# Attention kernel: sums of exponentials by a DMA transpose and VectorE sums instead of matmuls with ones

## The chip, the core and the metric

The kernel runs on one core of a Trainium2 chip. The metric is device time in microseconds (us) for one launch. TensorE (PE in the profile) does the matmuls, ScalarE (ACT) the exponentials, VectorE (DVE) elementwise work, sums and evacuations, GpSimd (POOL) some elementwise work, and SyncE (SP) issues most of the DMA transfers.

## The reference

The layer is group norm, one linear map to queries, keys and values, attention with 8 heads of 64 channels over 2304 positions, an output projection and a residual, for 4 images.

```python
b, c, h, w = 4, 512, 48, 48          # t = 2304 positions, d = 64
hn  = group_norm(x, 32 groups) * gn_scale + gn_bias
qkv = einsum('oc,bchw->bohw', qkv_w, hn) + qkv_b        # then float16
w   = softmax(einsum('bhct,bhcs->bhts', q * scale, k * scale), axis=-1)
a   = einsum('bhts,bhcs->bhct', w, v)
out = x + einsum('oc,bchw->bohw', proj_w, a) + proj_b
```

The softmax needs, for every head and query t, the sum over all 2304 keys s of exp(score). This change concerns only how that sum is formed.

## The kernel before

Two heads ("a pair") are worked on together: 4 images x 4 pairs = 16 pairs g. The queries of a pair are cut into 5 blocks j, four of 512 queries and one of 256: 80 blocks. A block's keys are worked through in steps of three score tiles: 6 steps for a block of 512, 3 for one of 256; 432 steps in all ("stream"). Scores are computed as keys x queries: the keys lie on the 128 partitions, the queries along the row. So the sum over keys is a sum over partitions plus a sum over tiles.

```python
P, D, QB, BURST, BEHIND = 128, 64, 512, 3, 2
ppool = tc.tile_pool(name="ppool", bufs=3)
work  = tc.tile_pool(name="work", bufs=2)
small = tc.tile_pool(name="small", bufs=2)
ps_s  = tc.tile_pool(name="ps_s", bufs=3, space=PSUM)
ps_av = tc.tile_pool(name="ps_av", bufs=1, space=PSUM)   # products with v, and the sums
ps_w  = tc.tile_pool(name="ps_w", bufs=1, space=PSUM)    # other work: q, k, v, projection

def scores(u):                       # one step: 6 matmuls and 3 exponentials
    pt = ppool.tile([P, BURST, 2, QB], F16, tag="p")
    for r in range(BURST):
        ps = ps_s.tile([P, 2, QB], F32, tag="ps")
        ...
                    nc.tensor.matmul(ps[:, h, ...], kt[rows, ...], qt[rows, o : o + n], ...)  # L932
        nc.scalar.activation(pt[:, r], ps, AF.Exp)                                            # L939

def values(u):                       # exponentials times v, two steps behind
    ...
                    nc.tensor.matmul(av[0][lo : lo + D, :n], vv[...], pt[:, r, h, ...], ...)  # L957
    if last and u is not stream[-1]:
        avx[g, j] = work.tile([P, QB], F32, tag="avx")
        nc.vector.tensor_copy(avx[g, j][:, :n], av[0][:, :n])                                 # L966

def add(u):                          # exponentials of the steps added up, elementwise
    ...
    t = acc[g, j][0]                 # [P, BURST, 2, QB] float16, one buffer
    nc.vector.tensor_tensor(t, before, pt, ALU.add)                                           # L986
    if last:
        for r in range(1, BURST):
            nc.vector.tensor_tensor(t[:, 0], t[:, 0], t[:, r], ALU.add)                       # L989
        acc[g, j] = [t[:, :1]]

def add_up(g, j, bank=None, more=False):        # sum over partitions by ones on TensorE
    sl = ps_av.tile([P, QB], F32, tag="av")     # (or the bank given)
    ...
            nc.tensor.matmul(sl[lo : lo + D, :n], ones16, t[:, r, h, ...], ...)               # L1009
    return sl

def rows(g, j, sl):                  # out of PSUM, and one row of each head to 128 partitions
    sx = work.tile([P, QB], F32, tag="rows")
    nc.vector.tensor_copy(sx[:, :n], sl[:, :n])                                               # L1025
    sm = small.tile([P, 2, QB // P], F32, tag="sums")
    for h in range(2):
        nc.sync.dma_start(sm[:, h, : n // P], sx[h * D : h * D + 1, :n])                      # L1028
    ...

def invert(g, j):
    nc.vector.reciprocal(inv[:, :, :per], sums[g, j][:, :, :per])                             # L1054
    nc.sync.dma_start(row[:, :n].rearrange("h (p i) -> p h i", i=per), inv[:, :, :per])       # L1056

def spread(g, j):                    # each head's row to its 64 partitions
    nc.sync.dma_start(ib[h * D : (h + 1) * D, :n], row[h : h + 1, :n].to_broadcast((D, n)))   # L1066

def divide(g, j):
    nc.gpsimd.tensor_tensor(atts[g][:, o : o + n], avx..., ibs..., ALU.mult)                  # L1073
```

The linear maps for later pairs and images and the projections of earlier images are cut into pieces, and `fill` puts them between the steps; each piece ends with an evacuation of its PSUM bank by VectorE (L719 for q and k, L768 for v, L864 for the projection). `fill` also gives VectorE statistics and normalization of the next image ("tasks"), with less room at the steps near a block's end. The order of issue, one turn for each step n, `block_at(m)` being the block that ended at step m:

```python
for n in range(end):
    while loads and loads[0][0] <= n:          # x, residuals, outputs, on SP
        loads.popleft()[1]()
    summed = block_at(n - BEHIND - 1)
    if summed:
        rows(*summed, add_up(*summed))
    scores(stream[n])
    if n > 0:
        add(stream[n - 1])
    if summed:
        fill(n)
    if n >= BEHIND:
        values(stream[n - BEHIND])
    if block_at(n - BEHIND - 2):
        check_sums(...); invert(...)           # check_sums: a range check of the sums on GpSimd
    if block_at(n - BEHIND - 3):
        spread(...)
    if block_at(n - BEHIND - 4):
        divide(...)
    if not summed:
        fill(n)
    ...                                        # the last three blocks are summed by add_up here and below
```

Of the kernel before, what the change touches and what calls it, by code (L numbers as in the profile page):

```python
# [12 lines left out]
F32 = mybir.dt.float32  # L13
F32R = mybir.dt.float32r
F16 = mybir.dt.float16
I32 = mybir.dt.int32
AF = mybir.ActivationFunctionType
ALU = mybir.AluOpType
AX = mybir.AxisListType
# [7 lines left out]
P = 128  # L27
# [6 lines left out]
BEHIND = 2  # L34
# [8 lines left out]
QB = 512  # L43
QBLOCKS = [(o, min(QB, T - o)) for o in range(0, T, QB)]
NQ = len(QBLOCKS)
# [422 lines left out]
def fast_path(  # L468
# [12 lines left out]
    nc = tc.nc  # L481
# [3 lines left out]
    xpool = ctx.enter_context(tc.tile_pool(name="xpool", bufs=1))  # L485
# [4 lines left out]
    work = ctx.enter_context(tc.tile_pool(name="work", bufs=2))  # L490
    small = ctx.enter_context(tc.tile_pool(name="small", bufs=2))
# [415 lines left out]


    open_sums = set()
    av, acc, pts, avx, sums, rowd, ibs = {}, {}, {}, {}, {}, {}, {}  # L910

    stream = []
    for g in range(NG):
# [54 lines left out]
    def add(u):  # L968

        g, j, k, last = u  # L970
        pt = pts[u]
        if k == 0:
            acc[g, j] = [pt]
            return
        if j >= NQ - 2 and g == NG - 1 and (last or j == NQ - 1):
            acc[g, j].append(pt)
            return
        before = acc[g, j][0]
        if k == 1:
            acc[g, j] = [  # L980
                work.tile(
                    [P, BURST, 2, QB], F16, tag="acc", bufs=1, name=f"acc_{g}_{j}"
                )
            ]
        t = acc[g, j][0]
        nc.vector.tensor_tensor(t, before, pt, ALU.add)  # L986
        if last:
            for r in range(1, BURST):
                nc.vector.tensor_tensor(t[:, 0], t[:, 0], t[:, r], ALU.add)  # L989
            acc[g, j] = [t[:, :1]]  # L990

    def add_up(g, j, bank=None, more=False):


        o, n = QBLOCKS[j]
        per = QB // n
        sl = bank
        if bank is None:
            sl = ps_av.tile([P, QB], F32, tag="av", name=f"sl_{g}_{j}")
        steps = [  # L1000
            (t, r, a)
            for t in acc.pop((g, j))
            for r in range(t.shape[1])
            for a in range(per)
        ]
        for i, (t, r, a) in enumerate(steps):
            for h in range(2):
                lo = h * D
                nc.tensor.matmul(  # L1009
                    sl[lo : lo + D, :n],  # L1010
                    ones16,
                    t[:, r, h, a * n : (a + 1) * n],
                    start=(i == 0 and (g, j) not in open_sums),
                    stop=(i == len(steps) - 1 and not more),
                )
        if more:
            acc[g, j] = []
            open_sums.add((g, j))
        return sl

    def rows(g, j, sl):

        o, n = QBLOCKS[j]
        sx = work.tile([P, QB], F32, tag="rows", name=f"slx_{g}_{j}")
        nc.vector.tensor_copy(sx[:, :n], sl[:, :n])  # L1025
        sm = small.tile([P, 2, QB // P], F32, tag="sums", name=f"sums_{g}_{j}")
        for h in range(2):
            nc.sync.dma_start(sm[:, h, : n // P], sx[h * D : h * D + 1, :n])  # L1028
        sums[g, j] = sm
        return sx  # L1030

    def divide_here(g, j, source, products, engine):
        o, n = QBLOCKS[j]
        inv = work.tile([P, QB], F32, tag="rows", name=f"inv_{g}_{j}")
        nc.vector.reciprocal(inv[:, :n], source[:, :n])
        engine.tensor_tensor(
            atts[g][:, o : o + n], products[:, :n], inv[:, :n], ALU.mult
        )

    def check_sums(g, j):  # L1040
        n = QBLOCKS[j][1]
        sm = sums[g, j][:, :, : n // P]
        ok = fine.rearrange("p (h i) -> p h i", h=2)[:, :, : n // P]
        for op, limit in ((ALU.is_ge, SUM_MIN), (ALU.is_le, SUM_MAX)):
            t = small.tile([P, 2, QB // P], F32, tag="in", name=f"in_{g}_{j}")
            t = t[:, :, : n // P]
            nc.gpsimd.tensor_scalar(t, sm, limit, None, op)  # L1047
            nc.gpsimd.tensor_tensor(ok, ok, t, ALU.mult)

    def invert(g, j):  # L1050
        n = QBLOCKS[j][1]
        per = n // P
        inv = small.tile([P, 2, QB // P], F32, tag="inv", name=f"inv_{g}_{j}")
        nc.vector.reciprocal(inv[:, :, :per], sums[g, j][:, :, :per])  # L1054
        row = dram.tile([2, QB], F32, tag="row", name=f"row_{g}_{j}")
        nc.sync.dma_start(  # L1056
            row[:, :n].rearrange("h (p i) -> p h i", i=per), inv[:, :, :per]
        )
        rowd[g, j] = row

    def spread(g, j):
        n = QBLOCKS[j][1]
        row = rowd.pop((g, j))
        ib = work.tile([P, QB], F32, tag="rows", name=f"ib_{g}_{j}")
        for h in range(2):
            nc.sync.dma_start(  # L1066
                ib[h * D : (h + 1) * D, :n], row[h : h + 1, :n].to_broadcast((D, n))
            )
        ibs[g, j] = ib

    def divide(g, j):
        o, n = QBLOCKS[j]
        nc.gpsimd.tensor_tensor(  # L1073
            atts[g][:, o : o + n],
            avx.pop((g, j))[:, :n],
            ibs.pop((g, j))[:, :n],
            ALU.mult,
        )
# [37 lines left out]
    def do_tasks(room):  # L1116
        while tasks and tasks[0][0] <= now[0] and room > 0:
            _, us, run = tasks.popleft()
            run()
            room -= us  # L1120
# [18 lines left out]
    def ready(b, j):  # L1139

        if b < B - 1:
            return BEHIND + 6
        return BEHIND + (4 if j == NQ - 3 else 5)

    def put_convert(b, j):
        end = ends[((b + 1) * NPAIR - 1) * NQ + j]
# [16 lines left out]
    for b in range(B):  # L1163
        g = b * NPAIR
# [118 lines left out]
    def fill(n):  # L1283

        idle = beside and beside[0][4] and not beside[0][4]()
        if ended(n - 1):
            room = 1.1 if idle else 0.0  # L1290
        elif ended(n - BEHIND - 1):
            room = 1.1 if idle else 0.5
        else:
            room = 2.4 if idle else 1.1
        do_tasks(room)
        rate, work = 0.0, 0.0
        for us, _, _, _, _, _, need in beside:
            work += us
            left = min(need * per_pair, len(stream) - 4) - n
            rate = max(rate, work / max(left, 1))  # L1300
        credit[0] = min(credit[0] + rate, 4.0)
        closed = False
        while beside:
            us, _, first, last, when, after, _ = beside[0]
            if after > n or (first and closed) or (when and not when()):
                break
            if us > 0.1 and credit[0] < us / 2:
                break
            issue()
            closed = closed or last  # L1310
# [11 lines left out]
    ended = lambda n: 0 <= n < len(stream) and stream[n][3]  # L1322
# [5 lines left out]
    def block_at(n):  # L1328

        return stream[n][:2] if ended(n) and n not in soon else None  # L1330

    for n in range(end):
        now[0] = n
        while loads and loads[0][0] <= n:
            loads.popleft()[1]()
        summed = block_at(n - BEHIND - 1)
        if summed:
            rows(*summed, add_up(*summed))
        wanted(stream[n][0])
        scores(stream[n])  # L1340
        if n > 0:
            add(stream[n - 1])
        if summed:

            fill(n)
        if n >= BEHIND:
            values(stream[n - BEHIND])
        if block_at(n - BEHIND - 2):
            check_sums(*block_at(n - BEHIND - 2))
            invert(*block_at(n - BEHIND - 2))  # L1350
        if block_at(n - BEHIND - 3):
            spread(*block_at(n - BEHIND - 3))
        if block_at(n - BEHIND - 4):

            divide(*block_at(n - BEHIND - 4))
        if not summed:
            fill(n)
        if n - BEHIND in soon:
            g, j = stream[n - BEHIND][:2]
            sx = rows(g, j, add_up(g, j))  # L1360
            if n - BEHIND == soon[1]:
                divide_here(g, j, sx, avx[g, j], nc.gpsimd)
        if n - BEHIND - 1 == soon[0]:
            check_sums(g, j)
            invert(g, j)
        if n - BEHIND - 2 == soon[0]:
            spread(g, j)
            divide(g, j)
    g, b, j = NG - 1, B - 1, NQ - 1
    n = QBLOCKS[j][1]  # L1370
# [9 lines left out]
    add_up(g, j, sl)  # L1380

    every = fine.shape[1] + n
    fines = work.tile([P, QB], F32, tag="rows", name="fines")[:, :every]
    ok = work.tile([P, QB], F32, tag="avx", name="ok")[:, :n]
    nc.scalar.copy(fines[:, :n], sl[:, :n])
    nc.gpsimd.tensor_scalar(ok, fines[:, :n], SUM_MIN, None, ALU.is_ge)
# [83 lines left out]
```

## Time and profile before

| | before |
|---|---|
| time, median of 3 runs | 1618.3 us (1618.05 to 1618.92) |
| span of the profiled run | 1617.1 us, 28315 instructions |
| mean granted TensorE clock | 0.999 |
| DMA | 82.11 MB, mean 51 GB/s |
| exponentials, L939 | 1296 x 1027 ns = 1231.9 us of ScalarE |
| additions of exponentials, L986 | 349, about 1.8 us each, 623.5 us of VectorE |
| matmuls with ones, L1009 | 234, 33.96 us in the records of TensorE |

The busy shares are those of the records: matmuls overlap, so the time that a record of a matmul covers is longer than what the matmul adds to the chain of work that ended last. In the chain, each stretch of time belongs to one instruction only. In a row of the groups, the first numbers are busy time and the mean duration of one, and behind the second bar stands the idle time of the engine just before them and what ended it. In the DMA issues, the last number is the median time from issue to landing.

### The profile page before, as it was taken

The page shows a single profiled execution, that of the slowest core. Times are in us where ns is not written, and L with a number is a line of the kernel's source. Part 1 is how long each engine was busy: PE and PEld are TensorE (multiplying, and loading weights), DVE is VectorE, ACT ScalarE, POOL GpSimd, SP SyncE. Part 2 cuts the span into 40 slices and gives each one's busy share as a digit, 9 for nine tenths or more (in the row PEclk, how much of TensorE's full clock was granted, in tenths as well). Part 3 has the DMA queues.
Part 4 walks back from the last instruction along what each step waited for, and adds up shares of the span by engine and source line. Part 5 has one row for each costly group of instructions (what it writes and reads, how often), then busy time and mean ns, then how long its engine had stood idle before and what let it go on. Part 6 is the DMA issues. An engine that isn't in the chain of part 4 may idle for free.

```text
span 1617.1 us, 28315 instructions
## 1 busy us (share of the span) xinstructions
PE 1583.4 (98%) x11500; PEld 695.5 (43%) x11500; DVE 1136.2 (70%) x1302; ACT 1282.8 (79%) x1398; POOL 298.4 (18%) x419
## 2 busy tenths in 40 slices
PE   6999999999999999999999999999999999999996
PEld 2533434443333534555333353455533334434544
DVE  6267668866666678986666666898666666767775
ACT  3077777888888888888887887887888888888894
POOL 1001102211121222212111121111211131111211
PEclk9999999999999999999999999999999999999999
DMA  7002020000000023511000002352100000016424
GB/s 221 1 14 66 11 64 24 18 14 11 14 18 14 12 65 118 154 54 28 14 11 18 14 12 61 100 158 73 31 14 12 14 18 15 15 24 191 121 62 132
DMA packets 94898, 82.11 MB, mean 51 GB/s; under 512 B 50852, under 2 KB 60964, under 8 KB 94756
## 3 DMA queue, kind: packets, MB, share of 16 engines
q1 hardware_dynamic: 92724, 78.35, 17.3%
q8 instruction: 92, 1.51, 0.4%
q10 hardware_dynamic: 1904, 1.84, 0.4%
q14 instruction: 50, 0.41, 0.1%
q0 software_dynamic: 128, 0.01, 0.0%
HBM read 60.70 MB, written 19.17 MB: 49 GB/s over the span
## 4 chain that ended last, share of the span: by engine, by line
PE 91%; ACT 4%; issue 2%; DVE 1%; DMA 1%; POOL 0%; SPq 0%; ACTq 0%; DVEq 0%; POOLq 0%
PE pqk L709 29%; PE ps L932 19%; PE av L957 19%; PE pv L760 16%; PE pr L837 7%; ACT p L939 3%; PE ps L709 1%; PE sl L1009 1%; ACT a L831 1%; DMA x<-x_dram 1%; DVE acc L986 0%; DMA sums<-slx 0%; DVE r L860 0%; DMA row<-inv 0%; DMA ib<-row 0%
## 5 line engine op out<-in xcount | busy, mean ns | idle before, releaser
L939 ACT ACTIVATE p<-ps 128x1024 f16<-128x1024 f32 x1296 | 1231.9, 1027 | 299.9 <-PE ps L932 299.3
L986 DVE TENSOR_TENSOR acc<-acc,p 128x3072 f16<-128x3072 f16 x270 | 485.3, 1798 | 75.5 <-ACT p L939 74.7
L709 PE MATMUL pqk<-x,wqkv 128*64 128x512 f32 (+1 forms) x2464 | 519.3, 551 | 0.0
L932 PE MATMUL ps<-q,k 64*128 64x512 f16 (+1 forms) x2880 | 359.5, 358 | 6.2 <-ACT p L939 5.3
L957 PE MATMUL av<-p,v 128*64 128x512 f16 (+1 forms) x2880 | 361.0, 364 | 0.4 <-DVE slx L1025 0.3
L760 PE MATMUL pv<-wqkv,x 128*64 128x256 f32 x2304 | 268.6, 380 | 0.0
L709 PEld LDWEIGHTS pqk<-x,wqkv 128*64 128x64 f32 x2464 | 168.9, 137 | 224.2 <-issue 166.8
L1047 POOL TENSOR_SCALAR in<-sums 128x8 f32<-128x8 f32 (+1 forms) x158 | 116.6, 738 | 795.0 <-DMA sums<-slx 788.7
L932 PEld LDWEIGHTS <-k 64*128 64x128 f16 x2880 | 107.3, 94 | 286.1 <-issue 238.1
L957 PEld LDWEIGHTS <-v 128*64 128x64 f16 x2880 | 131.9, 109 | 210.8 <-issue 166.6
L1073 POOL TENSOR_TENSOR att<-avx,ib 128x512 f16<-128x512 f32 (+1 forms) x78 | 120.0, 1539 | 450.4 <-DMA ib<-row 406.3
L760 PEld LDWEIGHTS pv<-wqkv,x 128*64 128x64 f32 x2304 | 160.1, 137 | 92.8 <-issue 4.5
L986 DVE TENSOR_TENSOR acc<-p,p 128x3072 f16<-128x3072 f16 x79 | 138.2, 1749 | 0.0
L837 PE MATMUL pr<-a,whi 128*128 128x512 f32 (+1 forms) x312 | 122.2, 399 | 4.6 <-DVE r L860 3.2
L837 PE MATMUL pr<-a,wlo 128*128 128x512 f32 (+1 forms) x312 | 114.4, 373 | 0.0
L989 DVE TENSOR_TENSOR acc<-acc 128x1024 f16<-128x1024 f16 x156 | 108.4, 695 | 5.4
L719 DVE TENSOR_SCALAR q<-pqk,bqkv 128x512 f16<-128x512 f32 (+1 forms) x79 | 55.0, 696 | 80.4 <-PE pqk L709 79.8
L719 DVE TENSOR_SCALAR k<-pqk,bqkv 128x512 f16<-128x512 f32 (+1 forms) x75 | 52.2, 696 | 78.1 <-PE pqk L709 78.0
L768 DVE TENSOR_TENSOR v<-pv,bv 128x512 f16<-128x512 f32 x72 | 49.7, 691 | 81.1 <-PE pv L760 80.9
L966 DVE COPY avx<-av 128x512 f32<-128x512 f32 (+1 forms) x79 | 50.6, 641 | 66.4 <-PE av L957 66.4
L864 DVE SCALAR_TENSOR_TENSOR r<-pr,bproj,r 128x512 f32<-128x512 f32 (+1 forms) x80 | 54.9, 694 | 43.6 <-PE pr L837 43.0
L837 PEld LDWEIGHTS pr<-a,whi 128*128 128x128 f32 x312 | 58.5, 187 | 41.9 <-issue 18.7
(62 smaller groups left out, 448.8 us busy)
## 6 DMA issues: line engine op xcount, KB each, us to landing
r<-x_dram SPq DMA_DIRECT2D x72, 256.0 KB, 3.0
out_dram<-r SPq DMA_DIRECT2D x69, 256.0 KB, 2.1
ib<-row SPq DMA_DIRECT2D x126, 128.0 KB, 3.0
x<-x_dram SPq DMA_DIRECT2D x62, 256.0 KB, 4.3
x<-x_dram SPq DMA_DIRECT2D x16, 128.0 KB, 4.8
sums<-slx SPq DMA_DIRECT2D x128, 2.0 KB, 2.1
ib<-row SPq DMA_DIRECT2D x30, 64.0 KB, 3.0
wqkv<-qkv_wT_dram SPq DMA_DIRECT2D x2, 768.0 KB, 6.9
```

The costliest lines, as they stand in the source:

```text
L709: nc.tensor.matmul(pw[0][lo : lo + D, :n], wqkv[:, c, w0 + lo : w0 + lo + D], hn[b, c, j], start=(c == 0), stop=(c == NC - 1),)
L719: nc.vector.tensor_scalar(qk[g][part][:, o : o + n], pw[0][:, :n], bqkv[:, col : col + 1], SCALE, ALU.add, ALU.mult,)
L760: nc.tensor.matmul(pw[0][lo : lo + D, a, :], hn[b, c, i * P // QB][:, at + lo : at + lo + D], wqkv[:, c, 2 * C + half * C // 2 :][:, : C / ...
L837: nc.tensor.matmul(ps[:, :n], w[:, c, bass.ts(m, P)], at32[b, j, c], start=(i == 0), stop=(i == len(steps) - 1),)
L864: nc.vector.scalar_tensor_tensor(xt[:, i], places[i], bias, xt[:, i], ALU.add, ALU.add)
L932: nc.tensor.matmul(ps[:, h, a * n : (a + 1) * n], kt[rows, bass.ts(i, P)], qt[rows, o : o + n], start=True, stop=True,)
L939: nc.scalar.activation(pt[:, r], ps, AF.Exp)
L957: nc.tensor.matmul(av[0][lo : lo + D, :n], vv[b, pr // 2][:, i, pr % 2 * P + lo : pr % 2 * P + lo + D], pt[:, r, h, a * n : (a + 1) * n], ...
L986: nc.vector.tensor_tensor(t, before, pt, ALU.add)
L989: nc.vector.tensor_tensor(t[:, 0], t[:, 0], t[:, r], ALU.add)
L1047: nc.gpsimd.tensor_scalar(t, sm, limit, None, op)
L1073: nc.gpsimd.tensor_tensor(atts[g][:, o : o + n], avx.pop((g, j))[:, :n], ibs.pop((g, j))[:, :n], ALU.mult,)
```

## The change

The sum over keys is no longer formed by TensorE. VectorE joins the three partial sums of a block in a tile of its own ("joined", 128 x 1024, float16). One DMA on the SP queue transposes it, 128 x 128 piece by piece, into the tile "turned", so that the queries lie on the partitions and the keys along the row. VectorE sums along the row. For the last three blocks the matmuls with ones stay. With this change the block's sums no longer need the PSUM bank of the products with v, and the VectorE copy out of PSUM and two small transfers go; the reciprocals lie differently on the partitions, and are written to DRAM with a row split as (i p) and not (p i). The steps at which the sums, the spread and the division are issued move, the room for tasks is set differently near a block's end, and the pieces of projection that need the result start one step later. Some tiles change their buffers.

```diff
@@ add
         nc.vector.tensor_tensor(t, before, pt, ALU.add)
         if last:
+            whole = work.tile([P, 1, 2, QB], F16, tag="joined", bufs=1, name=f"j_{g}_{j}")
+            so_far = t[:, 0]
             for r in range(1, BURST):
-                nc.vector.tensor_tensor(t[:, 0], t[:, 0], t[:, r], ALU.add)
-            acc[g, j] = [t[:, :1]]
+                nc.vector.tensor_tensor(whole[:, 0], so_far, t[:, r], ALU.add)
+                so_far = whole[:, 0]
+            acc[g, j] = [whole]
@@ new
+    def turn(g, j):
+        t = work.tile([P, 2 * QB // P, P], F16, tag="turned", bufs=1, name=f"t_{g}_{j}")
+        (whole,) = acc.pop((g, j))
+        nc.sync.dma_start(t, whole.rearrange("p a h q -> p (a h q)"), transpose=True)
+        turned[g, j] = t
+
+    def sum_up(g, j):
+        o, n = QBLOCKS[j]
+        sm = small.tile([P, 2, QB // P], F32, tag="sums", name=f"sums_{g}_{j}")
+        t = turned[g, j].rearrange("p (h a i) k -> p h i a k", h=2, i=n // P)
+        if n == QB:
+            nc.vector.tensor_reduce(sm, t[:, :, :, 0], AX.X, ALU.add)
+        else:
+            for h in range(2):
+                nc.vector.tensor_reduce(sm[:, h, : n // P], t[:, h], AX.XY, ALU.add)
+        sums[g, j] = sm
@@ rows, divide_here, spread, fines: buffers
-        sx = work.tile([P, QB], F32, tag="rows", name=f"slx_{g}_{j}")
+        sx = work.tile([P, QB], F32, tag="turned", bufs=1, name=f"slx_{g}_{j}")
-        inv = work.tile([P, QB], F32, tag="rows", name=f"inv_{g}_{j}")
+        inv = xpool.tile([P, QB], F32, tag=f"x{2 * (j - NQ) + 5}_1", name=f"inv_{g}_{j}")
-        ib = work.tile([P, QB], F32, tag="rows", name=f"ib_{g}_{j}")
+        ib = work.tile([P, QB], F32, tag="ib", bufs=1, name=f"ib_{g}_{j}")
@@ invert
-        nc.sync.dma_start(
-            row[:, :n].rearrange("h (p i) -> p h i", i=per), inv[:, :, :per]
-        )
+        if (g, j) in turned:
+            for h in range(2):
+                nc.sync.dma_start(
+                    row[h, :n].rearrange("(i p) -> p i", p=P), inv[:, h, :per]
+                )
+        else:
+            nc.sync.dma_start(
+                row[:, :n].rearrange("h (p i) -> p h i", i=per), inv[:, :, :per]
+            )
@@ ready
         if b < B - 1:
-            return BEHIND + 6
-        return BEHIND + (4 if j == NQ - 3 else 5)
+            return BEHIND + 7
+        return BEHIND + (4 if j == NQ - 3 else 6)
@@ fill
-        elif ended(n - BEHIND - 1):
-            room = 1.1 if idle else 0.5
+        elif ended(n - 4):
+            room = 1.1 if idle else 0.3
@@ the loop over steps
-        summed = block_at(n - BEHIND - 1)
-        if summed:
-            rows(*summed, add_up(*summed))
+        if block_at(n - 3):
+            turn(*block_at(n - 3))
         wanted(stream[n][0])
         scores(stream[n])
         if n > 0:
             add(stream[n - 1])
-        if summed:
-            fill(n)
         if n >= BEHIND:
             values(stream[n - BEHIND])
-        if block_at(n - BEHIND - 2):
-            check_sums(*block_at(n - BEHIND - 2))
-            invert(*block_at(n - BEHIND - 2))
-        if block_at(n - BEHIND - 3):
-            spread(*block_at(n - BEHIND - 3))
-        if block_at(n - BEHIND - 4):
-            divide(*block_at(n - BEHIND - 4))
-        if not summed:
-            fill(n)
+        fill(n)
+        if block_at(n - 4):
+            sum_up(*block_at(n - 4))
+            check_sums(*block_at(n - 4))
+            invert(*block_at(n - 4))
+        if block_at(n - 6):
+            spread(*block_at(n - 6))
+        if block_at(n - 7):
+            divide(*block_at(n - 7))
...
```

## What was predicted, and why

> **What bounds the kernel now.** I read the busy shares first, then the chain of work that ended last, then that chain in a stretch of sixty microseconds in the middle.
>
> ```profile
> PE 1583.4 (98%) x11500; PEld 695.5 (43%) x11500; DVE 1136.2 (70%) x1302; ACT 1282.8 (79%) x1398; POOL 298.4 (18%) x419
> PE 91%; ACT 4%; issue 2%; DVE 1%; DMA 1%; POOL 0%; SPq 0%; ACTq 0%; DVEq 0%; POOLq 0%
> PE pqk L709 29%; PE ps L932 19%; PE av L957 19%; PE pv L760 16%; PE pr L837 7%; ACT p L939 3%; PE ps L709 1%; PE sl L1009 1%; ACT a L831 1%; DMA x<-x_dram 1%; DVE acc L986 0%; DMA sums<-slx 0%; DVE r L860 0%; DMA row<-inv 0%; DMA ib<-row 0%
> ```
>
> TensorE is 91% of the chain, so a matmul that goes away shortens the end almost one for one, as long as no other engine makes TensorE wait in its place. The matmuls that this change removes are `PE sl L1009`: 1% of the chain (1.1% in the finer answer, about 17.8 us of 1617.1). That is the ceiling of the intended gain. The chain from 900 to 960 us shows one such place whole, at the end of one block of 512 queries:
>
> ```profile
> 908.62 0.76 PE ps L932 x6
> 909.37 0.77 PE av L957 x6
> 910.14 1.72 PE pqk L709 x8
> 911.86 0.22 PE sl L1009 x2
> 912.07 0.75 PE ps L932 x6
> 912.83 1.87 PE pqk L709 x8
> 914.69 0.65 PE av L957 x6
> ```
>
> An ordinary step (scores, values, one piece of other work) is 0.76 + 0.77 + 1.72 = 3.25 us. The step with the sums is 0.22 + 0.75 + 1.87 + 0.65 = 3.49 us. So the two matmuls with ones cost 0.22 us by themselves and 0.24 us with the other order of the pieces in that step. ScalarE needs 3 x 1027 ns = 3.08 us a step for its exponentials, so it is close behind TensorE but does not set the pace here.
>
> **What the Trainium skill says.** (1) "VectorE: DVE Perf Modes", section "The perf-mode tier table", says that `tensor_reduce` has only the slowest mode, one element a cycle, whatever the type. The trace of before has one such instruction, too small to tell (264 elements, 418 ns), so I size the new ones from two rows of another instruction that reads one input, below. (2) "DMA: Bandwidth & Descriptors", section "Latency and other measured facts", gives a DMA transpose 261 GB/s in an unfavourable layout and 350 to 400 in a good one. For 128 x 1024 x 2 B = 256 KB that makes 0.7 to 1.0 us of transfer, an estimate. (3) "VectorE: DVE Perf Modes", section "The three transpose paths", gives 1309 ns for one 128 x 128 transpose by DMA; eight of them in a row would be 10.5 us, also an estimate. The two pages are ten times apart, and no transpose by DMA is in the trace of before. (4) "DMA: Bandwidth & Descriptors", section "Rules for kernel authors", says that a last dimension that isn't contiguous becomes one descriptor for each element. The new write of the reciprocals is of that kind: 2 x 512 pieces of 4 B, where before four neighbours went together.
>
> **The change part by part.** There are 80 blocks (16 pairs of heads x 5). The listing of instructions of the changed kernel keeps the matmuls with ones for three of them and takes them from 77; the pieces of other work in each of the 432 steps are the same in kind and number as before, so nothing else changes in what TensorE computes.
>
> *TensorE, removed.* The chain shows 0.22 us for a block of 256 queries as well (four small matmuls). 77 x 0.22 = 16.9 us, and about 0.02 us for the order of the pieces in each, 77 x 0.02 = 1.5 us. Together 18 us. From it I take about 1 us, because from 1460 to 1585 us ScalarE is on 18.8% of the chain, and there a shorter TensorE step partly turns into a wait for the exponentials. On the path: -17 us.
>
> *VectorE, exchanged.* Rows of before:
>
> ```profile
> L1025 DVE COPY slx<-sl 128x512 f32<-128x512 f32 x64 | 43.8, 684 | 19.1 <-PE sl L1009 19.1
> L608 DVE BATCH_NORM_STATS2 st<-x 128x6 f32<-128x512 f32 x64 | 41.2, 678 | 5.2 <-DMA x<-x_dram 5.2
> L1025 DVE COPY slx<-sl 128x256 f32<-128x256 f32 x15 | 6.3, 417 | 5.8 <-PE sl L1009 5.8
> L608 DVE BATCH_NORM_STATS2 st<-x 128x6 f32<-128x256 f32 x16 | 6.3, 412 | 0.0
> ```
>
> The two statistics rows give (678 - 412) / 256 = 1.04 ns an element and 146 ns of fixed cost. A sum over 1024 elements then takes 146 + 1024 x 1.04 = 1.21 us, and for a block of 256 queries two sums of 512 take 2 x 0.68 = 1.36 us. Added: 62 x 1.21 + 15 x 1.36 = 95 us. Removed: the copy of the sums out of PSUM, 62 x 0.68 + 15 x 0.42 = 48 us. The join of the three partial sums costs the same as before (two instructions of 0.7 us), it only writes another tile. VectorE goes from 1136 to about 1183 us, 73%. By count this lies beside TensorE.
>
> *The chain from sums to division, moved.* It was: copy, two small transfers, reciprocal, row to DRAM, spread over partitions, division on GpSimd. It becomes: transpose, sum, reciprocal, two scattered row writes, spread, division. The division stands in the seventh step behind the block's last one, where it stood in the sixth, and the projections that use the result start one step later as well (9 for 8 in the first three batches, 8 for 7 for most of the last). GpSimd is 18% busy and the division isn't on the chain in the middle of the kernel: nothing on the path.
>
> *Whether the transpose is ready in time.* In the block above, the last VectorE join ends at 909.3 us. The transpose is issued on the SP queue, in its program order at the start of the third step after the block's last one, though SP may run ahead to that point. The sum stands on VectorE behind the evacuation of the fourth step, which there ended at 919.4 us. So the transfer has between 7.5 us (issued at 911.9) and 10 us (issued at 909.3). The nearest relatives in the DMA issues are plain transfers of the same 256 KB:
>
> ```profile
> r<-x_dram SPq DMA_DIRECT2D x72, 256.0 KB, 3.0
> x<-x_dram SPq DMA_DIRECT2D x62, 256.0 KB, 4.3
> ```
>
> With 3 to 5 us the transpose is in time in a quiet stretch. After a short block (3 steps) the tile "joined", of which there is one, is needed for the next join some 5 us after the issue, also enough. What I charge is for the three stretches where x, residuals and outputs share the queue (640 to 700, 1030 to 1100, 1460 to 1500 us, DMA share 0.5 to 0.7): some 12 blocks lie there, and I put 0.2 us on each, 2 to 3 us in all, as a guess.
>
> Sum: 1618.3 - 17 + 2 = 1603 us.
>
> **The rivals.** *First, the transfer is late and VectorE waits.* VectorE takes its work in order, so a late transpose holds back the evacuations that free TensorE's banks. Before has this once, at 1039 us, when a small transfer of sums stood behind 1 MB of x:
>
> ```profile
> 1039.41 0.35 SPq L1028
> ...
> 1039.81 4.51 DMA sums<-slx
> ...
> 1044.41 0.15 DVE inv L1054
> ...
> 1046.20 2.13 PE pr L837 x8
> ```
>
> VectorE waited 2.17 us for it, and TensorE was busy 18.21 of 20 us from 1040 to 1060: about 1.8 us lost for one wait. If the slow estimate of 10.5 us holds for every transpose, VectorE would wait 1 to 3 us at most of the 77 blocks, TensorE would lose about 1 to 2 us each, and the time would be 1680 to 1760 us. For it speaks the page's 1309 ns; against it, that a single small transfer is mostly fixed cost (2.1 us to landing for 2 KB here), which eight pieces of one DMA needn't pay eight times. If only the dense stretches suffer, 12 blocks x 1.8 us = 22 us eat the gain: about 1622 us.
>
> *Second, VectorE becomes the bound in the dense stretches.* From 600 to 700 us it is busy 87.35 of 100 us. Four or five blocks fall in it, each with 0.5 us more: about 90 us. That is under TensorE's 99, and lateness of a microsecond is caught up in the next step. It would cost a few us at most: 1605 to 1610.
>
> *Third, the gain is hidden.* If ScalarE took over, no change would show: 1618. But 3.08 us a step against 3.25 leaves room, and the chain between 130 and 500 us has no ScalarE in it at all. I don't think so.
>
> **Range and chances.** The ceiling of 18 us with no loss makes 1600 and lies near the lower end; nothing in the change can give over 2% (32 us), since all the matmuls with ones together are 17.8 us. The upper side is open: dense stretches that lose half the gain or all of it are 1610 to 1620, the slow transpose is far above. I hold 1603 us, 1597 to 1616 us for 8 in 10, and 2% for faster by over 2%, 89% for within 2%, 9% for slower by over 2%.
>
> **What the profile of the changed kernel would show.** Right: L1009 with only the last three blocks' matmuls, about 17 us less TensorE busy time, TensorE still 97 to 98% of the span, the transposes landing in under 7 us, the sums over rows about 1.2 us each with next to no idle time before them. Wrong: idle time of VectorE before the sum or the join, ended by the DMA of the transpose, and TensorE waits on VectorE's evacuations that follow it; or a transpose that lands in 8 us or more. The prediction falls if transposes hold up VectorE in quiet stretches too, or if the scattered row writes make the reciprocals so late that GpSimd's division and the projections behind it wait.

## The result, and the profile after

The changed kernel takes 1776.61 us (1772.27 to 1782.82), the kernel before, measured beside it, 1618.61 us: a ratio of 1.0976, 95% interval [1.0951, 1.1]. 158 us were lost where 15 were expected to be gained. The page of the changed kernel, busy shares and chain:

```profile
PE 1609.6 (91%) x11316; PEld 700.4 (39%) x11316; DVE 1193.8 (67%) x1317; ACT 1285.4 (72%) x1398; POOL 340.2 (19%) x419
PE 62%; DMA 21%; DVE 10%; issue 3%; ACT 2%; SPq 2%; POOL 0%; DVEq 0%; ACTq 0%; POOLq 0%
PE pqk L709 20%; PE ps L932 12%; PE av L957 12%; PE pv L760 11%; DMA t<-j 10%; DMA r<-x_dram 7%; PE pr L837 6%; DVE acc L986 3%; DMA row<-inv 2%; DMA x<-x_dram 2%; DVE sums L1038 2%; ACT p L939 1%; PE ps L709 1%; DVE r L864 1%; SPq L1082 1%
```

TensorE fell from 91% to 62% of the chain, and DMA rose from 1% to 21%. The matmuls went as planned (11500 to 11316 instructions), but TensorE now idles for 1777.9 - 1609.6 = 168 us where it idled 34, and its mean granted clock is 0.959 where it was 0.999. Three kinds of transfer stand in the chain: the transposes (t<-j), the residuals (r<-x_dram), the row of reciprocals (row<-inv). The residuals weren't touched by the change. The waits of the changed kernel (first number us in all, then times, then the longest), of SP, VectorE and TensorE:

```profile
SPq L1096 <- DMA row<-inv: 584.1, 113, 10.5
```

```profile
DVE r L864 <- DMA r<-x_dram: 84.9, 12, 10.7
...
DVE sums L1041 <- DMA t<-j: 61.6, 13, 9.3
...
DVE sums L1038 <- DMA t<-j: 4.2, 3, 1.9
```

```profile
PE pr L837 <- DVE r L864: 93.1, 15, 9.1
```

SP waits 584 us for the row of reciprocals to reach DRAM (the kernel before waited 129.8 us at the same place). VectorE waits for residuals, and for the transposes only at the 15 short blocks (L1041), next to never at the 62 long ones (L1038): a short block's transpose is issued right behind the row write of the block before it, as at 902.67 us below. TensorE waits behind VectorE's evacuations. The SP queue itself, in a quiet part of the changed kernel (start, duration of issue, what):

```profile
881.41 0.92 SPq L1082 DMA_DIRECT2D row<-inv  x2
890.43 2.01 SPq L1096 DMA_DIRECT2D ib<-row  x2
892.54 1.26 SPq L1029 DMA_TRANSPOSE t<-j  x1
901.70 0.93 SPq L1082 DMA_DIRECT2D row<-inv  x2
902.67 1.23 SPq L1029 DMA_TRANSPOSE t<-j  x1
910.79 2.92 SPq L1096 DMA_DIRECT2D ib<-row  x2
```

Between the row's issue and the spread that needs it lie 9 us both times; the first time nothing else is issued on SP in between. The chain of the changed kernel there, and where residuals are loaded, tells how long transfers took:

```profile
881.83 10.14 DMA row<-inv
...
892.54 6.06 DMA t<-j
...
902.67 11.08 DMA t<-j
```

```profile
677.88 2.60 DMA r<-x_dram
...
684.14 12.57 DMA r<-x_dram
...
696.80 0.76 DVE r L864
```

A transpose issued when the row has landed, behind the spread, takes 6 us; one issued right behind a row write 11 us. A residual of 256 KB, issued 0.6 us after a row write, takes 12.6 us; another one, in the same stretch with no row write in flight, takes 2.6 us, about as before (3.0 us at the median). So the suspicion falls on the row write and not on the transpose.

### The profile page after: what moved, and what is told of

It reads as the page before. It is cut to its first block, busy times and chain, and to the rows that moved or that the text cites. A ratio compares the mean times of both kernels' runs of the same rounds, so it can differ in the third digit from the quotient of the medians.

```text
span 1777.9 us, 27819 instructions
## 1 busy us (share of the span) xinstructions
PE 1609.6 (91%) x11316; PEld 700.4 (39%) x11316; DVE 1193.8 (67%) x1317; ACT 1285.4 (72%) x1398; POOL 340.2 (19%) x419
## 4 chain that ended last, share of the span: by engine, by line
PE 62%; DMA 21%; DVE 10%; issue 3%; ACT 2%; SPq 2%; POOL 0%; DVEq 0%; ACTq 0%; POOLq 0%
PE pqk L709 20%; PE ps L932 12%; PE av L957 12%; PE pv L760 11%; DMA t<-j 10%; DMA r<-x_dram 7%; PE pr L837 6%; DVE acc L986 3%; DMA row<-inv 2%; DMA x<-x_dram 2%; DVE sums L1038 2%; ACT p L939 1%; PE ps L709 1%; DVE r L864 1%; SPq L1082 1%
## 5 line engine op out<-in xcount | busy, mean ns | idle before, releaser
L709 PE MATMUL pqk<-x,wqkv 128*64 128x512 f32 (+1 forms) x2464 | 526.8, 558 | 29.3 <-DVE k L719 14.8
L932 PE MATMUL ps<-q,k 64*128 64x512 f16 (+1 forms) x2880 | 366.0, 364 | 6.6 <-ACT p L939 5.9
L709 PEld LDWEIGHTS pqk<-x,wqkv 128*64 128x64 f32 x2464 | 172.8, 139 | 253.3 <-issue 166.4
L1103 POOL TENSOR_TENSOR att<-avx,ib 128x512 f16<-128x512 f32 (+1 forms) x78 | 122.4, 1570 | 714.6 <-DMA ib<-row 669.2
L837 PE MATMUL pr<-a,whi 128*128 128x512 f32 (+1 forms) x312 | 134.5, 437 | 96.1 <-DVE r L864 93.1
L1071 POOL TENSOR_SCALAR in<-sums 128x8 f32<-128x8 f32 (+1 forms) x158 | 92.2, 584 | 655.3 <-DVE sums L1038 437.5
L957 PEld LDWEIGHTS <-v 128*64 128x64 f16 x2880 | 126.6, 109 | 215.3 <-issue 176.3
L864 DVE SCALAR_TENSOR_TENSOR r<-pr,bproj,r 128x512 f32<-128x512 f32 (+1 forms) x80 | 54.8, 693 | 131.8 <-DMA r<-x_dram 84.9
L837 PE MATMUL pr<-a,wlo 128*128 128x512 f32 (+1 forms) x312 | 125.6, 408 | 0.0
L837 PEld LDWEIGHTS pr<-a,whi 128*128 128x128 f32 x312 | 65.6, 210 | 136.5 <-DVE r L864 74.2
L1072 POOL TENSOR_TENSOR fine<-fine,in 128x8 f32<-128x8 f32 (+1 forms) x158 | 114.5, 725 | 13.2
```

What stands on the lines that cost most here:

```text
L709: nc.tensor.matmul(pw[0][lo : lo + D, :n], wqkv[:, c, w0 + lo : w0 + lo + D], hn[b, c, j], start=(c == 0), stop=(c == NC - 1),)
L837: nc.tensor.matmul(ps[:, :n], w[:, c, bass.ts(m, P)], at32[b, j, c], start=(i == 0), stop=(i == len(steps) - 1),)
L864: nc.vector.scalar_tensor_tensor(xt[:, i], places[i], bias, xt[:, i], ALU.add, ALU.add)
L932: nc.tensor.matmul(ps[:, h, a * n : (a + 1) * n], kt[rows, bass.ts(i, P)], qt[rows, o : o + n], start=True, stop=True,)
L957: nc.tensor.matmul(av[0][lo : lo + D, :n], vv[b, pr // 2][:, i, pr % 2 * P + lo : pr % 2 * P + lo + D], pt[:, r, h, a * n : (a + 1) * n], ...
L1103: nc.gpsimd.tensor_tensor(atts[g][:, o : o + n], avx.pop((g, j))[:, :n], ibs.pop((g, j))[:, :n], ALU.mult,)
```

## The experiments

Theory A: the write of the reciprocals as 1024 pieces of 4 bytes holds up SP and the transfers behind it. Theory B: the transposes themselves do it. Later two more theories were needed for a smaller remainder.

### e1_row16: the row in 16-byte pieces

```diff
 # shortened
-        if (g, j) in turned:  two writes, row[h, :n].rearrange("(i p) -> p i", p=P)
+        nc.sync.dma_start(row[:, :n].rearrange("h (p i) -> p h i", i=per), inv[:, :, :per])
@@ divide
-        atts[...], avx[:, :n], ib[:, :n]
+        atts[...].rearrange("c (i p) -> c i p", p=P), avx[:, :n].rearrange("c (i p) -> c i p", p=P),
+        ib.rearrange("c (p i) -> c i p", i=n // P)
```

> The changed kernel, but the reciprocals are written to the DRAM row in the order in which they lie, (p i), one write of 16-byte (or 8-byte) pieces as in the kernel before, and the division on GpSimd undoes the order by strided views. Theory A (the scattered write of 1024 pieces of 4 bytes, about 9 us each time, holds the SP queue and the DMA engines): the write lands in 2 to 3 us again, the waits of VectorE on residuals and transposes fall from about 150 us to under 20 us, and the time is 1600 to 1615 us. Theory B (the transposes themselves, 5.5 us and more, are the cause): the waits on transposes stay, and the time is above 1700 us.

Measured: 1618.37 us, ratio to before 1.0001 [0.9992, 1.0009]. The DMA issues of e1_row16 (median us to landing last):

```profile
t<-j SPq DMA_TRANSPOSE x77, 3.1
...
row<-inv SPq DMA_DIRECT2D x63, 4.0 KB, 2.3
```

All of the 158 us are gone with this one edit, and the transposes, all 77 still there, land in 3.1 us. VectorE waits 4.4 us for residuals and transposes where it waited 150.7 us. Theory B falls. But the time missed theory A's range too, by 3 us: the gain of the removed matmuls doesn't show.

### e2_before_scatter: the scattered write alone

```diff
 # in the kernel before
-        nc.sync.dma_start(row[:, :n].rearrange("h (p i) -> p h i", i=per), inv[:, :, :per])
+        for h in range(2):
+            nc.sync.dma_start(row[h, :n].rearrange("(i p) -> p i", p=P), inv[:, h, :per])
```

> The kernel before (sums by ones on TensorE, no transpose), but its reciprocals are written to DRAM by two writes with a row split as (i p), 1024 pieces of 4 bytes, as in the changed kernel; the reciprocals land at other queries' places, so the output is not the reference's. Theory A (the scattered write is the cause): the write takes 8 to 10 us, residuals behind it come late, and the time is 1660 to 1760 us. Theory B (the transposes are the cause): 1617 to 1630 us.

Measured: 1759.88 us, ratio 1.0879 [1.0862, 1.0896]. The write alone, with no transpose in the kernel, costs 142 of the 158 us, in theory A's range. SP waits 637.9 us for it, and VectorE 86.3 us for the small transfers of sums behind it.

### e3_row_act and e4_row_twice: queue, and number of pieces

```diff
 # shortened; e3: two functions; the write one step later, on ScalarE's queue
-            nc.sync.dma_start(row[h, :n].rearrange("(i p) -> p i", p=P), inv[:, h, :per])
+            nc.scalar.dma_start(row[h, :n].rearrange("(i p) -> p i", p=P), inv[:, h, :per])
 # e4: each write a second time
+            nc.sync.dma_start(spare[h, :n].rearrange("(i p) -> p i", p=P), inv[:, h, :per])
```

> The changed kernel, but its scattered row writes are issued one step later on ScalarE's queue, not on SP. Theory A1 (the write's pieces occupy the DMA engines, whatever the queue): transfers from SP still come late, time above 1700 us. Theory A2 (only the order in the SP queue holds the others back): residuals and transposes no longer wait, the time is 1600 to 1650 us. Theory B (transposes alone): about 1777 us, since nothing changes for them.

> The changed kernel with each scattered row write issued twice, the second time to a DRAM tile that nothing reads. Theory A (the scattered write is the cause): the write takes about 18 us in place of 9, and at least another 150 us are lost, 1900 us or more. Theory B (the transposes are the cause): within 20 us of 1777 us.

Measured: e3 1690.59 us, 1.0442 [1.0426, 1.0459]; e4 1788.55 us, 1.1052 [1.1032, 1.1072]. Neither met its numbers. In e3 the loss halves: residuals on SP no longer stand behind the writes in their own queue (VectorE waits 38.1 us for them, not 84.9), but SP waits even longer for the row before it can issue the spread (873.3 us). But the order in the queue isn't all of it. One place of e3 (lines left out between):

```profile
382.04 1.23 SPq L1029 DMA_TRANSPOSE t<-j  x1
...
382.28 1.11 ACTq L1092 DMA_DIRECT2D row<-inv  x2
...
391.58 1.28 DVE L1041 TENSOR_REDUCE sums<-t 128x2 f32<-128x512 f16 x2 [1.19 <-DMA t<-j]
```

The transpose stands in SP's queue and the row write, 0.24 us later, in ScalarE's, and still the sum that waits for the transpose starts only 9.5 us after the transpose's issue. So a row write delays transfers of another queue too, as theory A1 says; how much of e3's 72 us that makes, and how much the spread's wait, this run doesn't separate. e4 contradicts the simple picture that 1024 pieces cost 9 us and 2048 cost 18: twice the pieces cost 12 us of time and not 150, and the row lands no later (issued at 303.51 us, its spread at 313.05). The changed kernel's own trace says the same: a short block's row has half the pieces, and in the first four of them 8.3 to 9.4 us lie between the row's issue and the spread. So the cost doesn't follow the number of pieces, which led to the next two.

### e7_spare_dense and e8_spare_apart: what is slow in the write

```diff
 # in e1_row16, behind the row's write
+            spare = dram.tile([2, QB], F32, tag="spare")          # e8: [2, QB, 16]
+            for h in range(2):
+                nc.sync.dma_start(spare[h, :n].rearrange("(i p) -> p i", p=P), inv[:, h, :per])
+                                                                  # e8: spare[h, :n, 0]
```

> e1_row16, and beside it the two scattered writes of 4-byte pieces of each block to a DRAM tile that nothing reads: no instruction waits for them, they are only in the SP queue and the DMA engines. Theory A1 (the pieces block transfers issued behind them): residuals and transposes come late, 1680 to 1760 us. Theory A3 (the harm in the changed kernel came only from the spread waiting in the SP queue for the write): 1618 to 1635 us.

> As e7_spare_dense, but in the tile that nothing reads the 4-byte pieces lie 64 bytes apart. If the number of pieces sets the cost: as e7_spare_dense within 15 us. If the writes of neighbouring 4-byte pieces hinder each other: at least half of the loss of e7_spare_dense is gone.

Measured: e7 1737.03 us, 1.0733 [1.0716, 1.0749]; e8 1626.64 us, 1.0046 [1.0031, 1.0062]. In e7 no instruction needs the added writes, and yet 119 us over e1_row16 are lost: the writes hold up what stands behind them (VectorE waits 73.2 us for residuals, 45.9 us for transposes of short blocks). So theory A3, that the spread's wait in the queue does all of it, falls: SP's waits at the spread, for the row and the added writes together, are 68.6 us, less than the 107.3 us of e1_row16. In e8 the same number of 4-byte pieces (both traces have 183620 packets under 512 B), only 64 bytes apart, costs 8 us. The landing of the extra writes in e8:

```profile
spare<-inv SPq DMA_DIRECT2D x124, 2.0 KB, 3.1
```

So it isn't small pieces as such: pieces of 4 bytes are slow when they lie next to each other in DRAM. Pieces of 16 bytes that lie next to each other are not (2.3 us in e1). Neighbours come from different partitions in all these writes, so whether that matters no run tells. That e4's two tiles could be written side by side would fit, but isn't shown. By what means neighbours hinder each other no run here shows.

### e5_divide_early and e6_plain_divide: where the gain went

In e1_row16 TensorE's records are down to 1570.2 us (13 less than before), but its idle time is up from 33.7 to 47.4 us. A place where it waits, in e1_row16 (lines left out between):

```profile
320.17 3.12 POOL L1099 TENSOR_TENSOR att<-avx,ib 128x512 f16<-128x512 f32 x1 [3.05 <-DMA ib<-row]
...
321.93 1.91 DVE L991 TENSOR_TENSOR j<-acc 128x1024 f16<-128x1024 f16 x1
323.87 0.69 DVE L991 TENSOR_TENSOR j<-j,acc 128x1024 f16<-128x1024 f16 x1
...
324.48 0.68 DVE L768 TENSOR_TENSOR v<-pv,bv 128x512 f16<-128x512 f32 x1
...
325.22 1.95 PE L760 MATMUL pv<-wqkv,x 128*64 128x256 f32 x16 [0.31 <-DVE v L768]
```

The first join runs 1.91 us beside GpSimd's division, the second 0.69 us by itself; the evacuation of v behind them comes late, and TensorE waits 0.31 us. The Trainium skill, "SBUF — State Buffer", section "Who interferes with whom", says that a VectorE instruction with two inputs in SBUF contends with a GpSimd instruction that reads SBUF; these lines agree.

```diff
 # e5, from e1: spread at n - 5 (was n - 6), divide at n - 6 (was n - 7), ready() as before
 # e6, from e1: the division with plain views again
```

> e1_row16 with the spread in the fifth and the division in the sixth step behind a block's last one, and the projections' start, as in the kernel before. In e1_row16 the time was that of before although 31 us of matmul records were gone; its first join took 1203 ns on average in place of 693, and in the trace the slow ones overlap the division on GpSimd, which in the seventh step falls on the next block's join. Theory C (this meeting of division and join makes VectorE late and gives the gain back): the first join is about 700 to 800 ns again and the time is 1600 to 1608 us. Theory D (VectorE simply has too much work with the sums over rows): 1614 to 1620 us, as e1_row16.

> The changed kernel with the row written in 16-byte pieces as in e1_row16, but the division left as it was, so that the reciprocals meet other queries' values and the output is not the reference's. It tells what the strided views of the division cost. If they are what slows the join (theory C1): the division takes about 1690 ns and not 1952, the first join about 820 ns, and the time is 1602 to 1610 us. If only the step in which it runs counts (C2): within 3 us of 1618 us.

Measured: e5 1625.58 us, 1.0049 [1.0035, 1.0063]; e6 1611.49 us, 0.9963 [0.9949, 0.9977]. e5 missed: its first join still takes 1214 ns. A place in GpSimd's program doesn't set when it runs; the landing of the spread does, and that hardly moved (in the place above the division starts at 319.34 us, after 320.17 in e1). Why e5 is 7 us slower than e1 I haven't settled; its chain from 1000 to 1100 us runs through transposes (5.9%), residuals (4.2%) and rows (4.0%), which suggests that the earlier wait in the SP queue holds up the rest. In e6 the division takes 1702 ns, as expected, and 7 us of time are gained; so the strided views cost that much, though the time is 1.5 us above the range of C1. That they cost it because a longer division meets more of VectorE's work is likely and not shown. But the first join still takes 1084 ns where 820 were expected: the meeting itself remained.

### e12_step_earlier and e14_join_mixed: moving the meeting

```diff
 # e12, from e1; the start of the projections and the room for tasks also move one step
-        turn: block_at(n - 3)   sum_up, check_sums, invert: n - 4   spread: n - 6   divide: n - 7
+        turn: block_at(n - 2)   sum_up, check_sums, invert: n - 3   spread: n - 5   divide: n - 6
 # shortened; e14, from e12: plain row and division; order changed in the second join
+            nc.vector.tensor_tensor(whole as "x (b i p) -> x b i p",
+                                    t[:, 0] and t[:, 2] as "x (b p i) -> x b i p", ALU.add)
```

> e1_row16 with the whole chain one step earlier: transpose in the second, sum and reciprocal in the third, spread in the fifth and division in the sixth step behind a block's last one, the projections' start as in the kernel before. e5_divide_early moved only the issue of spread and division, and the division's moment didn't move, since it comes when the spread has landed: the chain of sum, row and spread must start earlier. Theory C (the division on GpSimd meets the step in which the next block's addition and join stand, VectorE's fullest): the first join falls from 1203 ns to under 850, TensorE's waits on evacuations by VectorE shrink, and the time is 1600 to 1610 us. Theory D (too much work on VectorE): 1615 us or more.

> As e12_step_earlier, but the order of the queries is changed in VectorE's second join (strided reads), so that row, spread and division are plain. If the strided division is what still costs in e12: 2 to 6 us under e12. If the slower join, on the step that is fullest for VectorE, costs more: 3 to 15 us over e12.

Measured: e12 1610.71 us, 0.9958 [0.9944, 0.9971]; e14 1620.50 us, 1.0015 [1.0008, 1.0021]. The page and the groups of e12:

```profile
PE 1565.3 (97%) x11316; PEld 683.2 (42%) x11316; DVE 1196.2 (74%) x1317; ACT 1282.8 (80%) x1398; POOL 381.0 (24%) x419
```

```profile
L991 DVE TENSOR_TENSOR j<-acc 128x1024 f16<-128x1024 f16 x78 | 60.2, 771 | 2.7
```

The first join is at 771 ns, inside theory C's number, and 7.7 us of time came with it (the time is 0.7 us over the range given). The earlier start of the projections doesn't explain the gain by itself: e5 has it too and gained nothing. Nor has all of VectorE become faster: the long additions to a sum take 1831 ns (1817 in e1, 1798 before). e14, with the extra cost put in the join's own step (1225 ns for the second join, 692 in e12), loses 9.8 us, which fits a step in which VectorE has little slack before TensorE waits. TensorE's records are 18.1 us less than before, which is the predicted amount of work; 7.6 us of it reach the end.

### e15_ones_beside_projection: where the rest went

In e12 TensorE's idle time is 1607.6 - 1565.3 = 42.3 us, against 33.7 before. The stretches of e12 with projections (us, then busy time of TensorE, weight loads, VectorE, ScalarE and GpSimd, granted clock, DMA share, GB/s):

```profile
600.00:700.00 100.00, 95.85 (x620) 46.91 (x618) 87.55 (x116) 83.00 (x99) 23.52 (x26) 1.00 0.51 141
1000.00:1100.00 100.00, 96.41 (x604) 45.31 (x602) 91.80 (x116) 85.55 (x102) 21.25 (x26) 1.00 0.54 145
1400.00:1500.00 100.00, 96.28 (x618) 43.40 (x614) 73.22 (x73) 87.14 (x101) 23.14 (x27) 1.00 0.44 121
1500.00:1560.00 60.00, 57.37 (x350) 30.77 (x348) 47.46 (x52) 54.66 (x69) 14.55 (x16) 1.00 0.43 90
```

14.1 us of idle time lie in these 360 us; before it was 6.8 in the same ones. Elsewhere, away from start and end, TensorE is busy for 99 to 100 of 100 us.

```diff
+    by_ones = lambda n: 153 <= n < 172 or 270 <= n < 289 or n >= 388
     # blocks that end in these steps: rows(add_up(...)) at n - 3, the rest as in the kernel before
```

> e12_step_earlier, but for the blocks that end where projections are the other work (steps 153 to 171, 270 to 288 and from 388) the sums stay with ones on TensorE, as in the kernel before. In e12_step_earlier 18 us of matmul records are gone and 7.6 us of time; TensorE's idle time grew by 8.6 us, nearly all of it in these three stretches, where the chain runs through ScalarE and VectorE. If the sums over rows on VectorE and the transposes beside residuals and outputs cost that time there: 1602 to 1608 us. If the sums are not what costs it: 1610 to 1614 us, for some 17 blocks have their 0.22 us of TensorE back.

Measured: 1607.03 us, ratio to before 0.993 [0.9916, 0.9943], in the range given. Idle time in the four stretches falls to 8.6 us, although 12 blocks have their matmuls with ones back (65 transposes are left of 77). TensorE's records are 4.6 us more than in e12, and the time is 3.7 us less. So where projections run, the matmuls with ones were nearly free, and the transposes with VectorE's sums were not; which of these two costs the time, this run doesn't separate.

## Why the prediction was wrong

*TensorE, removed: right in work.* 18 us of matmul time were reckoned. e12 shows 1583.4 - 1565.3 = 18.1 us fewer in the records.

*The chain from sums to division, moved: this step failed.* It names "two scattered row writes", the text before it says that the row goes in 4-byte pieces, and the step then books "nothing on the path" for the whole chain. No duration was put on the new write; the old one, in 16-byte pieces, landed in 2.2 us. Measured, the new one takes 8 to 12 us. It was judged off the path because the division is; but it also holds up the transfers around it, and those, residuals and transposes, are on the path. e2 has this cost alone, 142 us; e1 takes it away, and 158 us with it. The prediction did name the row writes as a sign of being wrong, by another way: that GpSimd's division and the projections behind it would wait. GpSimd waited longer for the spread (669.2 us, before 406.3), but TensorE's projections waited for the evacuations behind late residuals (93.1 us). The place of the Trainium skill that was quoted, one descriptor for each element, is right (e2 has 52224 pieces more than the kernel before, and 53472 packets under 512 B more) and not enough: e8 has one descriptor for each element and loses 8 us.

*Whether the transpose is ready in time: right by itself.* 3 to 5 us were taken from plain transfers of that size; it is 3.1 us in e1, and VectorE waits 0.4 us for transposes there. In the changed kernel they came late because of the row writes. The estimate of 10.5 us doesn't hold here. The faster figure of 0.7 to 1.0 us is transfer alone and isn't contradicted.

*The first rival: right in form, wrong in cause and size.* Late transfers, VectorE waiting in order, TensorE behind it: that is what the chain shows. It was tied to a slow transpose, and given 1680 to 1760 us; the culprit was the row write, and the time 1777 us. One cost is missing in that rival: the clock, granted at 0.959 on average in place of 0.999. Of the 161 us between the two profiled spans, TensorE's idle time makes 168.3 - 33.7 = 134.6. The other 26 are records: 18 us less work, and yet 26 us more busy time (1609.6 against 1583.4), so the same matmuls took 44 us longer than in e12, at 0.999.

*VectorE, exchanged: right in instructions, short in consequence.* 1.21 us for the sum of 1024 was estimated; 1209 ns measured. But the guess of 2 us of loss where work is dense was too small even with the row write mended: e12 loses 10 of the 18 us, most of it in the stretches of the second rival, and e1 lost all. What was not seen is the step with addition, join and evacuation, in which VectorE has little slack, and GpSimd's division that can fall on it.

*The third rival: right, with a wrong number.* ScalarE didn't hide the gain. But 3 x 1027 ns = 3.08 us a step is too much, as is 1296 x 1027 ns in the table of before: the records of neighbouring exponentials overlap. Their busy time of 1231.9 us over 432 steps is 2.85 us a step, so ScalarE left more room than was reckoned.

## What to carry to other kernels

A transfer off the critical path is not free: ask what stands behind it in the same queue, and price every added or reshaped transfer by its pieces and their places at the far end, not by its bytes. When a reduction changes the layout of its result, keep the memory's order natural for the writer and undo the permutation in the views of a reader, if that reader has slack. Even then it isn't free: the strided division cost 7 us here, with GpSimd busy for 21% of the time. And before work is moved from the bounding engine to another, find the step in which the other has least slack: the average share (70% here) doesn't tell.

## What the runs showed of the hardware

- 4-byte pieces written next to each other in DRAM, neighbours from different partitions: 8 to 12 us for 1024 of them, and transfers issued right behind them landed after 9 to 14 us. The same pieces 64 bytes apart: 3.1 us at the median for a write of 512. In 16-byte pieces: 2.3 us for the whole row.
- A transpose by DMA of 128 x 1024 float16 from SBUF to SBUF lands in 3.1 us at the median, about as a plain load of that size (3.7 us for residuals in e1).
- After a wait of 5.19 us, the matmuls of a projection in the changed kernel started about 0.43 us apart (after the first), later ones 0.24 us:

```profile
1132.11 0.80 PE L837 MATMUL pr<-a,whi 128*128 128x512 f32 x1 [5.19 <-DVE r L864]
1132.71 0.63 PE L837 MATMUL pr<-a,wlo 128*128 128x512 f32 x1
1133.13 0.63 PE L837 MATMUL pr<-a,whi 128*128 128x512 f32 x1
...
1141.68 0.40 PE L837 MATMUL pr<-a,whi 128*128 128x512 f32 x1
1141.92 0.40 PE L837 MATMUL pr<-a,wlo 128*128 128x512 f32 x1
```

The granted clock was 0.50 from 1132 to 1134 us and 1.00 from 1140 to 1142 us. The Trainium skill, "TensorE: Matmul & The Clock Gate", section "Part 1: The HAM clock gate", says that TensorE falls to half its clock after an idle window of about 3.4 us; these lines and clocks agree. A wait so costs more than its length.
